# Forty single-row loads per step instead of twenty-four, in a gather-and-sum kernel on one Trainium2 core

## The chip, the cores and the metric

The kernel runs on one core of a Trainium2 chip. The metric is the device time of one execution in microseconds; the time before is the median of three executions. An execution that was recorded by the hardware profiler is one of them, and everything said of the profile below comes from it.

## The reference

A graph layer with two kinds of messages, a residual sum, and a layer norm. `x` has 50,000 rows of 128 float32 numbers, and there are 1,650,000 edges, sorted by `dst`. Every node has one edge to itself among them.

```python
Xs = X[src]
m_data = Xs @ W_data.T + b_data
m_ctrl = Xs @ W_control.T + b_control
msg = jnp.where((edge_types == 0)[:, None], m_data, m_ctrl)
agg = jax.ops.segment_sum(msg, dst, num_segments=X.shape[0])
out = jax.nn.relu(agg + (X @ W_self.T + b_self))
result = layernorm(x + out)          # over the last axis
```

## The kernel before

The edges are cut into `NBLK` blocks, in their order. A block has `Q = 2` steps, and a step has `R = 12` chunks of 128 edges. For a chunk, one indirect DMA of GpSimd (POOL, line 483) fetches the 128 source rows of `x` into an SBUF tile `y`; TensorE multiplies `y` with a one-hot matrix `oh` of 128 x 120 (60 nodes for each of the two edge types, line 502), and so sums the rows by node and type into a PSUM tile `acc`. The weights are multiplied in later, once per block (`layer`). That is float32, so each product is two weight loads and two matmuls in the trace.

A step takes more edges than its 12 x 128 = 1,536, in two ways, and both make a block longer and the number of blocks smaller:

- **Fillers.** An edge from a node to itself needs no gather, since the node's own row is there anyway (`xT`). Its place in a chunk is given to another edge, a filler. `F = 43` of these are taken in a step. VectorE (DVE) works out which place gets which filler (`fill`, lines 315 to 337; its tiles are 128 x 26 x `F`), and corrects the sums for the edges that were left out (`left_out_columns`, `_matrix`, `_numbers`, `_rows`).
- **Single rows.** `S = sum(TURNS) = 24` more edges of a step are fetched one row at a time, 512 bytes for each DMA, by the queues of SP and ACT (`single_rows`, line 457): 12 in each step for each queue, so 24 in each block for each queue. The tile is `yx`, with a row on each partition. They are the `S` rows of one more product in each step (line 508, 24 partitions x 120).

For single rows the queue first reads the row offsets from `at_x` into registers (`TENSOR_LOAD`, line 452), then for each row does a register `MOVE` and a DMA issue, both line 457. `LOADS` says in how many parts this is done in a block; a part has at most 32 rows for each queue. The rows of block `b + 2` are issued in block `b` (`AHEAD = 2`), on two semaphores, and `rows_fetched` makes PE wait for all of them before the product of line 508 in the first step of their block (line 466). There are four tiles for them (`ROW_SLOTS`).

The order on each engine is written out by hand (`manual_schedule`), in the loop over `b` at the end of `straight`. A block has four passes of six chunks, two in each step. The gathers have ten tiles (`SLOTS`) of one pass each, so GpSimd can be up to ten passes ahead of PE; it waits for PE to free a tile. In a block's program order, with `q` for the pass:

- SP: `xT` of block `b + 3` (line 408), every tenth block the edge lists (lines 167 to 172) and the fillers' lists (lines 300, 305), the single rows of block `b + 2`, and every second block two output stores (line 577).
- ACT: the single rows of block `b + 2`, and every second block the square root of two blocks' variances (`root`, line 563).
- DVE: `add` of the last step of block `b - 1` (line 518), `begin_sums` (531), `offsets` for `at_x` (437), `onehot` and `counts` of block `b + 2` (414, 422), then `fill` of block `b + 5`, `add` of the first step, `moments` of block `b - 1` and the rest.
- PE: pass 0, `left_out_columns` (344), pass 1 with lines 508 and 511, `layer` of block `b - 1` (537 to 541), `left_out_numbers` (360, 363), pass 2, pass 3 with 508 and 511.

If a step has fewer edges to itself than `F`, or if its nodes don't fit the one-hot matrix, a flag is set, and a second, general way of computing everything runs after the first.

Of the kernel before, what the change touches and what calls it, by code (L numbers as in the profile page):

```python
# [37 lines left out]
PASS = 6  # L38
B = 112
C = R * Q  # L40
F = 43
TURNS = (12, 12)
S = sum(TURNS)
LOADS = 1
BEGIN = (0, -(-Q * TURNS[0] // 4) * 4)
X = BEGIN[1] + -(-Q * TURNS[1] // 4) * 4
R1 = R + 1
# [3 lines left out]
CE = Q * SIZE  # L51
BE = CE + Q * (F + S)
NBLK = 2 + (E - CE) // BE
# [30 lines left out]
def plain(b):  # L84

    return b == 0 or b >= NBLK - 1
# [6 lines left out]
def straight(ctx, tc, c, x, x_t, edges_t, edges_f, src_x, dst_first, first_p, out):  # L93
# [35 lines left out]
                   allow_small_or_imprecise_dtypes=True)  # L129
    FILL = Q * F + C1  # L130
    small = keep_ps.tile([P, 2 * W + F + 2 * FILL + 2], F32, name="small")
    num_ps, rank_no_ps = small[:, :2 * W], small[:, 2 * W:2 * W + F]
    lists = [small[:, 2 * W + F + i * FILL:][:, :FILL] for i in range(2)]
    sums_at = [small[:Q * F, 2 * W + F + 2 * FILL + i:][:, :1] for i in range(2)]

# [282 lines left out]
    def counts(b):  # L418

        cnt = ohp.tile([P, Q, 2 * W], BF16, name="cnt")  # L420
        with nc.allow_low_precision(reason="whole numbers up to R1"):
            nc.vector.tensor_reduce(cnt, ohs[b].rearrange("p (q r) w -> p q w r", r=R1), AX.X, ALU.add)  # L422
        cnts[b] = cnt
# [15 lines left out]
    def part_of(n, part):  # L439

        return min(n, 32 * part)

    def single_rows(b, part):

        if part == 0:
            ys[b] = stp.tile([S, Q, D], F32, name="yx", bufs=ROW_SLOTS)
        both = []
        for j, (eng, dma) in enumerate(((SP, nc.sync), (ACT, nc.scalar))):
            n = Q * TURNS[j]
            k0, k1 = part_of(n, part), part_of(n, part + 1)  # L450
            at = BEGIN[j]
            _, rows = nc.values_load_multi_w_load_instructions(ats[b][0:1, at + k0:at + k1], engines=[eng], **RANGE)
            both.append([(dma, fetched[j][b % ROW_SLOTS], *divmod(k0 + k, TURNS[j]), sum(TURNS[:j]), row)
                         for k, row in enumerate(rows)])
        for pair in zip_longest(*both):
            for dma, sem, q, k, at, row in filter(None, pair):
                copy = dma.dma_start(ys[b][at + k:at + k + 1, q, :].bitcast(U8), x_bytes[:, bass.ds(row, ROW)])
                copy.then_inc(sem, 16)
                tc.no_tile_sem_insts.add(copy.ins.name)
                tc.add_to_no_dep_group(f"single{b}", copy.ins)  # L460

    def rows_fetched(b):

        times = len(range(b % ROW_SLOTS or ROW_SLOTS, b + 1, ROW_SLOTS))
        for j in range(2):
            wait = nc.tensor.wait_ge(fetched[j][b % ROW_SLOTS], 16 * Q * TURNS[j] * times)
        tc.declare_fence(wait.ins, group=f"single{b}")
# [89 lines left out]
    def pair(b):  # L557

        return range(b // 2 * 2, b + 1) if b % 2 == 1 or b == NBLK - 1 else ()
# [6 lines left out]
    def store(bs):  # L566
        mv = mvs.pop(bs[0] // 2)
        rstd = stp.tile([B, 2], F32, name="rstd")
        nc.vector.reciprocal(rstd[:, :len(bs)], sds.pop(bs[0] // 2)[:, :len(bs)])
        for i, b in enumerate(bs):  # L570
            o = stp.tile([B, D], F32, name="o", bufs=4)
            nc.vector.tensor_scalar(o, hs.pop(b), mv[:, i, 0:1], rstd[:, i:i + 1], op0=ALU.subtract, op1=ALU.mult)
            os_[b] = o
# [43 lines left out]
    for b in range(1, RAHEAD):  # L617
# [3 lines left out]
        if b < AHEAD:  # L621
            onehot(b)
            counts(b)
            for part in range(LOADS):
                single_rows(b, part)
        if b == 1:
            clear_sums()
    for b in range(NBLK + 1):
# [20 lines left out]
        for q, (step, ks) in enumerate(passes_of(b)):  # L649
# [21 lines left out]
            if q == 3 and b > 0 and pair(b - 1):  # L671
                store(pair(b - 1))
            if q < LOADS and not plain(b + AHEAD):
                single_rows(b + AHEAD, q)
# [336 lines left out]
```

## Time and profile before

| What | Value |
|---|---|
| Median of three executions | 17865.75 us (17860.93 to 17866.0) |
| Profiled execution, its own time | 17866.0 us |
| Its span, first to last instruction | 17864.2 us |
| Instructions in the span | 162923 |
| Blocks; span for each | 515; 34.69 us |
| DVE busy | 11010.2 us (62%) |
| POOL busy | 11675.7 us (65%) |
| PE busy, weight loads | 8518.6 us (48%), 7294.5 us (41%) |
| ACT busy | 79.5 us |
| DMA | 53 GB/s, 2 tenths of the 16 engines' time |

The profile lists the engines' busy time, the groups of instructions by source line, who waited for whom, and the order of time. Register, semaphore and DMA-issuing instructions aren't counted as busy: so SP has no busy time at all, and ACT almost none, though both issue DMAs for most of the span. What they do is seen in the order of time and in the instructions of their lines. A releaser "remote" means that the profile found no instruction that ended the wait. "issue" means that the engine waited for nothing the profile shows.

### The profile page before, as it was taken

How to read it: one execution, taken by the hardware profiler on the slowest of the kernel's cores; microseconds unless marked ns; L12 is line 12 of the kernel's file. 1: busy time of each engine (PE TensorE's matmuls, PEld its weight loads, DVE VectorE, ACT ScalarE, POOL GpSimd, SP SyncE). 2: the span in 40 equal slices, each digit the busy share in tenths (PEclk: the TensorE clock that was granted, in tenths of full speed). 3: DMA queues.
4: the chain of work that ended last, by engine and by line, in shares of the span. 5: the costliest groups of instructions: out<-in, count | busy, mean ns of one | idle time of the engine just before them, and what ended most of it. 6: DMA issues, size and time to landing. Idle time of an engine off the chain costs nothing.

```text
span 17864.2 us, 162923 instructions
## 1 busy us (share of the span) xinstructions
PE 8518.6 (48%) x36190; PEld 7294.5 (41%) x36191; DVE 11010.2 (62%) x13887; ACT 79.5 (0%) x264; POOL 11675.7 (65%) x12364
## 2 busy tenths in 40 slices
PE   3444444444444444444444444444444444444444
PEld 3444444444444444444444444444444444444444
DVE  6666666666666666666665656666665666666665
ACT  0000000000000000000000000000000000000000
POOL 6666666666666666666666666666666666666666
PEclk6555555555555555555555555555555555555555
DMA  2122221222122122222212222121221212122121
GB/s 55 52 53 52 53 53 52 53 52 53 52 53 53 52 53 53 52 53 52 53 52 53 53 52 53 52 54 52 53 53 52 53 52 53 52 53 53 52 53 49
DMA packets 604666, 938.00 MB, mean 53 GB/s; under 512 B 308795, under 2 KB 392578, under 8 KB 603676
## 3 DMA queue, kind: packets, MB, share of 16 engines
q0 software_dynamic: 395392, 810.40, 17.4%
q1 hardware_dynamic: 183222, 110.53, 2.4%
q10 hardware_dynamic: 25062, 6.55, 0.2%
q8 instruction: 295, 4.83, 0.1%
q14 instruction: 695, 5.69, 0.1%
HBM read 896.80 MB, written 29.71 MB: 52 GB/s over the span
## 4 chain that ended last, share of the span: by engine, by line
DVE 39%; another core or an unknown queue 30%; issue 17%; PE 13%; DVEq 1%; SPq 0%; DMA 0%; ACT 0%; ACTq 0%
DVE cnt L422 11%; PE acc L502 9%; DVE oh L414 8%; DVE new L321 3%; DVE m L318 3%; DVE v_new L325 3%; DVE old L334 2%; DVE sums L518 2%; PE acc L508 1%; PE po L541 1%; DVE h L548 1%; DVE st L550 1%; DVE by L337 1%; PE po L539 1%
## 5 line engine op out<-in xcount | busy, mean ns | idle before, releaser
L483 POOL DMA_INDIRECT y<-in_x,idx x12336 | 11656.9, 945 | 6148.3 <-issue 3460.1
L502 PEld LDWEIGHTS acc<-oh,y 128*128 128x128 f32 x24708 | 5473.5, 316 | 8928.2 <-issue 6942.1
L502 PE MATMUL acc<-oh,y 128*128 128x120 f32 x24708 | 6125.0, 413 | 5208.9 <-issue 5203.1
L518 DVE TENSOR_TENSOR sums<-acc,sums 128x180 f32 x1030 | 354.8, 344 | 4744.9 <-remote 4432.1
L422 DVE TENSOR_REDUCE cnt<-oh 128x240 bf16<-128x3120 f32 x515 | 3011.9, 5848 | 17.9
L414 DVE TENSOR_TENSOR oh<-col,small 128x3120 f32<-128x3120 f32 x515 | 1743.1, 3385 | 0.0
L344 PE MATMUL small<-ones_b,by 128*86 128x1 bf16 x513 | 84.0, 164 | 3418.4 <-issue 2299.4
L337 DVE TENSOR_REDUCE by<-old 128x86 bf16<-128x1118 f32 x513 | 1111.2, 2166 | 19.0 <-DVE old L334 1.3
L547 DVE COPY h<-po 112x128 f32<-112x128 f32 x515 | 147.6, 287 | 1378.8 <-remote 1020.1
L508 PE MATMUL acc<-oh,yx 24*128 24x120 f32 x2052 | 783.0, 478 | 81.9 <-issue 80.4
L318 DVE TENSOR_TENSOR m<-rk,small 128x1118 f32<-128x1118 f32 x513 | 677.0, 1320 | 18.0 <-issue 0.5
L321 DVE TENSOR_TENSOR new<-m,small 128x1118 f32<-128x1118 f32 x513 | 677.1, 1320 | 17.6
L325 DVE TENSOR_REDUCE v_new<-new 128x26 f32<-128x1118 f32 x513 | 675.8, 1317 | 17.6
L334 DVE TENSOR_TENSOR old<-m,small 128x1118 f32<-128x1118 f32 x513 | 672.7, 1311 | 0.0
L508 PEld LDWEIGHTS acc<-oh,yx 24*128 24x128 f32 x2052 | 502.5, 300 | 306.0 <-issue 300.3
L541 PE MATMUL po<-wmsgT,sums 128*112 128x128 f32 x2060 | 613.1, 453 | 0.0
L541 PEld LDWEIGHTS po<-wmsgT,sums 128*112 128x112 f32 x2060 | 448.8, 297 | 127.4 <-issue 126.6
L539 PE MATMUL po<-bias,sums 3*112 3x128 f32 x1030 | 391.9, 482 | 1.0 <-DVE sums L518 1.0
L538 PE MATMUL po<-wselfT,xT 128*112 128x128 f32 x1030 | 325.2, 419 | 0.0
L511 PE MATMUL acc<-cnt,to_row 128*128 128x60 bf16 x2060 | 288.7, 230 | 69.4 <-issue 69.0
L531 DVE TENSOR_TENSOR sums<-pl,sums 128x336 f32<-128x336 f32 x513 | 260.3, 507 | 83.5 <-issue 53.0
L267 PEld LDWEIGHTS <-ones_b 128*128 128x128 bf16 x624 | 78.7, 149 | 540.0 <-issue 528.5
(118 smaller groups left out, 3994.2 us busy)
## 6 DMA issues: line engine op xcount, KB each, us to landing
y<-in_x,idx POOLq DMA_INDIRECT x12336
yx<-in_x ACTq DMA_DIRECT2D x12312, 0.5 KB
yx<-in_x SPq DMA_DIRECT2D x12312, 0.5 KB
xT<-in_x_t SPq DMA_DIRECT2D x515, 56.0 KB
out<-o SPq DMA_DIRECT2D x515, 56.0 KB
vf_all<-vd SPq DMA_DIRECT2D x52, 430.0 KB
sdt<-in_edges_t SPq DMA_DIRECT2D x52, 390.0 KB
one_g<-in_src_x SPq DMA_DIRECT2D x52, 1.9 KB
```

The lines of the kernel that those rows point to most:

```text
L318: nc.vector.tensor_tensor(m, rk_g[g][:, i, :, None].to_broadcast([P, C1, F]), rank_no_ps[:, None, :].to_broadcast([P, C1, F]), op=ALU.is_e ...
L321: nc.vector.tensor_tensor(new.rearrange("p (q r) f -> p q r f", r=R1), m.rearrange("p (q r) f -> p q r f", r=R1), vf.rearrange("p (q f) -> ...
L325: nc.vector.tensor_reduce(v, new, AX.X, ALU.add)
L334: nc.vector.tensor_tensor(old, m, cb[:, :, None].to_broadcast([P, C1, F]), op=ALU.mult)
L337: nc.vector.tensor_reduce(by, old.rearrange("p (q r) f -> p q f r", r=R1), AX.X, ALU.add)
L414: nc.vector.tensor_tensor(oh, col_g[g][:, i, :, None].to_broadcast([P, C1, 2 * W]), num_ps[:, None, :].to_broadcast([P, C1, 2 * W]), op=AL ...
L422: nc.vector.tensor_reduce(cnt, ohs[b].rearrange("p (q r) w -> p q w r", r=R1), AX.X, ALU.add)
L483: copy = nc.gpsimd.indirect_dma_start(out=y[:r, k % PASS, :].bitcast(U8), out_offset=None, in_=x_rows, in_offset=bass.IndirectOffsetOnAxis ...
L502: nc.tensor.matmul(acc[:, :2, :].rearrange("p t w -> p (t w)"), y[:r, k % PASS, :], ohs[b][:r, column(k), :], start=k == of_step[0], stop= ...
L508: nc.tensor.matmul(acc[:, :2, :].rearrange("p t w -> p (t w)"), ys[b][:, q, :], ohs[b][:S, q * R1 + R, :], start=False, stop=True)
L518: nc.vector.tensor_tensor(part, accs.pop((b, q)), part, op=ALU.add)
L541: nc.tensor.matmul(po, a[:, t, :B], c["wmsgT"][:, t * D:(t + 1) * D], start=False, stop=t == 1)
```

## The change

Three constants change. Nothing else does; all shapes follow from them.

```diff
-F = 43
-TURNS = (12, 12)
+F = 42
+TURNS = (20, 20)
 S = sum(TURNS)
-LOADS = 1
+LOADS = 2
```

What follows from them:

- A step takes 1,536 + 42 + 40 = 1,618 edges instead of 1,536 + 43 + 24 = 1,603, and a block 3,236 instead of 3,206. `NBLK = 2 + (E - CE) // BE` goes from 515 to 510.
- Each of the two queues issues 40 single rows in a block instead of 24, and reads their offsets in two parts, 32 and 8, instead of one of 24. The first part is issued after pass 0 in the program's order, the second after pass 1.
- The product of line 508 has 40 partitions instead of 24. `at_x` has 80 numbers instead of 48.
- The tiles of `fill` have 128 x 26 x 42 elements instead of 128 x 26 x 43.

## The prediction

> **What bounds the kernel now.** I read the page first. No engine is full: DVE 62%, POOL 65%, PE 48%. So I asked for POOL's waits, since the gathers are the work that the blocks are made of.
>
> ```profile
> L483 POOL DMA_INDIRECT y<-in_x,idx x12336 | 11656.9, 945 | 6148.3 <-issue 3460.1
> ```
> ```profile
> POOL y L483 <- issue: 3465.3, 11355, 1.9
> POOL y L483 <- remote: 2186.4, 692, 4.9
> POOL y L483 <- PE acc L502: 220.9, 122, 10.9
> ```
>
> A gather costs 0.945 us and 0.30 us of issue behind it, 1.247 us from start to start. A block's 24 take 29.9 us, of the 34.69 us that a block lasts (17864.2 / 515). The other 4.8 us are waits, for PE to free a tile of `y`. So PE is late, although it is idle for half of the span. The order of time shows why:
>
> ```profile
> 8063.99 0.36 PE L502 MATMUL acc<-oh,y 128*128 128x120 f32 x1 [1.74 <-issue]
> 8065.39 0.36 PE L502 MATMUL acc<-oh,y 128*128 128x120 f32 x1 [1.04 <-issue]
> ...
> 8077.19 2.90 PE L502 MATMUL acc<-oh,y 128*128 128x120 f32 x12
> ```
>
> There are two paces. In the third line 12 matmuls take 2.90 us, with their weight loads beside them; in the first two, one comes every 1.4 to 2.1 us, and PE waits for nothing that the profile names. The same is seen on the queues of the single rows:
>
> ```profile
> 8002.29 2.69 ACTq L457 DMA_DIRECT2D yx<-in_x  x8
> ```
> ```profile
> 8008.37 7.00 SPq L457 DMA_DIRECT2D yx<-in_x  x5
> ```
>
> Eight rows in 2.69 us, 0.335 us each; or five in 7.00, 1.40 us each. Instruction by instruction, PE, SP and ACT then go in steps of 0.70 us, and a row is two of them, `MOVE` and issue (a `MOVE` of 0.029 us takes 0.70). What holds them isn't told by the profile. Adding up the stretches in which one of the three goes at that step gives some 12,860 us, 72% of the span, 25.0 us of a block. They end 2 to 4 us after POOL stops and begin again some 5 us after it goes on, so the slow pace goes with running gathers. Here POOL had stopped, PE came free at 8075, and this is POOL's next gather:
>
> ```profile
> 8077.05 0.94 POOL L483 DMA_INDIRECT y<-in_x,idx  x1 [4.62 <-PE acc L502]
> ```
>
> Last I read the queue that the change loads, SP, in the order of time (two blocks of it) and by its waits.
>
> ```profile
> 8154.80 25.00 SPq L457 DMA_DIRECT2D yx<-in_x  x24
> 8180.50 0.00 SPq L408 DMA_DIRECT2D xT<-in_x_t  x1
> 8180.52 0.33 SPq L305 DMA_DIRECT2D vf_all<-vd  x1
> 8182.70 32.14 SPq L457 DMA_DIRECT2D yx<-in_x  x24
> 8217.34 2.55 SPq L577 DMA_DIRECT2D out<-o  x2
> ```
> ```profile
> SPq L577 <- DVE o L572: 1068.3, 94, 35.9
> SPq L408 <- remote: 478.8, 115, 22.9
> ```
>
> SP is never counted as busy, and is nearly full. A run of 24 rows takes 26.5 us in the mean of all 513, so 1.106 us for a row. All of SP's waits together are 1,825 us, 3.5 us of a block; for the other 31.1 us it is issuing. Of these 4.6 us are not rows (`xT`, stores, register loads, lists). ACT is less full: 20.2 us for 24 rows, and it waits 12.3 us of a block in front of the square root.
>
> **The change, part by part.**
>
> *Fewer blocks.* 510 instead of 515: 5 x 34.69 = 173 us less, 0.97%, if a block lasted as long as before.
>
> *42 fillers.* Lines 318, 321, 325, 334 (1.32 us each) and 337 (2.17 us) are 1/43 shorter: 0.17 us of DVE in a block. DVE is busy for 21.4 us of 34.7 and waits 4,432 us at line 518 alone; I cost it at nothing. If DVE were the bound, it would be 510 x 0.17 = 87 us less.
>
> *The product of line 508 with 40 partitions.* With 24 partitions its weight load takes 0.300 us, and line 502's with 128 takes 0.316. Partitions cost nothing here: zero, at most 4 x 0.016 us of PE in a block.
>
> *`at_x` with 80 numbers on one partition.* 0.198 us for 48 now; line 225, the same operation with 260, takes 0.298. So +0.02 us in a block, beside DVE's waits: nothing.
>
> *The offsets in two parts.* Line 452 takes 1.42 us on SP (median) for 24 registers; line 401 reads 8 in 0.777. That is 0.04 us for a register and 0.45 us for the load. 32 and 8 are then 1.74 + 0.78 = 2.52 us: 1.1 us more on SP in a block. ACT (1.67 us now) gets about as much. The ends are 0.78 us (one more load of 8) and 1.42 (a second load of 24).
>
> *Sixteen more rows in a block on each queue.* On SP the floor is 16 x 0.335 = 5.4 us, the present mean 16 x 1.106 = 17.7 us, the slow pace 16 x 1.40 = 22.4 us. SP has 3.5 us to spare. Even at the floor 5.4 + 1.1 = 6.5 us don't fit: SP becomes the engine that sets the end. At the floor a block needs 31.1 + 6.5 = 37.6 us, at the present mean 31.1 + 17.7 + 1.1 = 49.9 us.
>
> The value is nearer to the floor. When SP is late, PE waits at line 466, ahead of line 508. Behind it in PE's queue stand `layer`, `left_out_numbers` and passes 2 and 3; DVE waits for them at lines 518 and 547, and POOL for their tiles. So POOL stops, and the time added to a block is time without gathers, which has the fast pace. POOL's 29.9 us of gathers stay, and with them some 25.0 us of slow pace in a block. In these SP issues 25.0 / 1.40 = 17.9 rows. The other 22.1 take 22.1 x 0.335 = 7.4 us, and what isn't rows takes 4.6 + 1.1 = 5.7. Together 25.0 + 7.4 + 5.7 = 38.1 us. The waits of SP go, since they are for things (`o`, a free `xT`) that are long there when SP is the late one. ACT's rows need at its mean price 40 x 0.84 + 2.8 = 36.5 us, just less. Whatever small wait stays, I add 0.4 us: 38.5 us.
>
> There is a buffer: SP's last row of a block is issued 49.5 us (median; never under 26.8) before PE's product that uses it. It delays the effect by one or two blocks of 510 and takes nothing off the sum. The bytes are no term: 32 rows are 16 KB in a block, beside 24 gathers of 64 KB. `xT` is issued over 70 us ahead, so SP's other transfers come into no trouble first.
>
> The sum: 510 x 38.5 = 19,635 us, 1,770 above the profiled execution's 17,866.0, which stands 0.25 us from the median of the runs. I take 19,640.
>
> Two rules of the Trainium skill pull in opposite directions here. *DMA: Bandwidth & Descriptors*, section Issuing engines are not separate DMA queues, says that the sequencer's time to start a DMA "is usually small relative to the DMA itself"; by that the rows cost nothing and the sum would be -173 us. *Perfetto Trace Analysis*, section What "DMA-bound" means, counts a solid track of DMA slices on the issuing sequencer as a bound of its own; that speaks against the change, and SP's 31.1 us of 34.7 are of that kind.
>
> **The rivals.**
>
> *The rows are hidden (faster).* One mechanism: the slow pace shrinks, so that SP fits 40 rows into the block it has. The point is a mean price of (34.7 - 4.6 - 1.1) / 40 = 0.725 us for a row, against 1.106 now; ACT, at 0.84 for the same instructions, shows that such prices occur. Then POOL and PE go on as before: 17,866 - 173 = 17,690, or with DVE's part 17,600. Against it: nothing in the change slows the gathers, and SP goes slowly whenever they run. 0.06.
>
> *The slow pace is a limit on the number of instructions.* If PE, SP and ACT share something with a fixed rate, a block costs by its instructions: 316 now, and 64 more with the moves and issues, +20%. 34.69 x 1.20 x 510 = 21,260. For it: the free stretches are shorter the more SP and ACT issue in them. Against it: PE goes at 0.70 us also where SP and ACT issue nothing (8057 to 8075). 0.20.
>
> *The price of a row stays.* If slow stretches go on while POOL waits, a block takes up to 49.9 us: 25,450. Stretches end within 4 us of POOL's stop, against it. 0.10.
>
> *SP absorbs part*, because the slow stretches are fewer with longer stops: 35 to 36 us, 17,850 to 18,360. 0.03.
>
> *The change doesn't do what it says*: a step with fewer than 42 edges to itself, or with over 60 nodes, would start the general way, far slower. Counted from the inputs, the least is 43 and the most nodes 55, so it stays out. 0.01.
>
> **How the numbers follow.** The main case has 0.60. Its own range is 36.1 us (the slow pace is a tenth shorter and nothing waits) to 40.5 us (half of SP's present waits stay). The range reaches from its low end, 18,400, over the second rival's 21,260 to 22,500, where part of the third lies; outside are the first rival and most of the third, less than 2 in 10. A measurement of this kernel tells 0.2% (36 us) from no change. Faster 0.06; same 0.01, from the partial case; slower 0.93.
>
> **What the profile after should show.** 508 runs of 40 rows on SP with 20,320 rows on each queue and 12,240 gathers. SP's waits fall from 1,825 us to under 600. Runs of 40 rows on SP take 30 to 33 us, so 0.75 to 0.85 us a row. POOL's waits for tiles rise from 4.8 to 8 or 9 us of a block, and PE waits ahead of line 508 for the rows. DVE's busy time falls by 1 to 2%. I am wrong if SP still has waits of 3 us in a block, if POOL waits no longer than before, or if the rows' mean price is still 1.1 us.

## The result, and the profile after

| | before | after |
|---|---|---|
| Median | 17864.68 us (4 executions, 17860.93 to 17866.0) | 19067.91 us (4 executions, 19051.4 to 19087.19) |
| Profiled execution, own time and span | 17866.0, 17864.2 us | 19051.4, 19049.7 us |
| Blocks, span for each | 515, 34.69 us | 510, 37.35 us |
| Instructions in the span | 162923 | 194872 |
| DVE, POOL, PE busy | 11010.2, 11675.7, 8518.6 us | 10857.1, 11573.3, 6914.5 us |

The changed kernel is slower: 1.0674 times the time before, with a 95% interval of 1.0656 to 1.0693. Five blocks fewer would have brought 173 us; each of the 510 that are left takes 2.66 us more. Three groups of the page after, with the idle time ahead of each:

```profile
L483 POOL DMA_INDIRECT y<-in_x,idx x12216 | 11549.2, 945 | 7415.0 <-issue 3349.5
...
L508 PE MATMUL acc<-oh,yx 40*128 40x120 f32 x2032 | 643.8, 408 | 9148.8 <-issue 6185.7
...
L315 DVE COPY small<-vf_all 128x84 f32<-128x84 f32 x508 | 123.7, 243 | 2194.2 <-DMA vf_all<-vd 1026.0
```

The second of them before the change:

```profile
L508 PE MATMUL acc<-oh,yx 24*128 24x120 f32 x2052 | 783.0, 478 | 81.9 <-issue 80.4
```

A gather still takes 945 ns. What grew is the idle time ahead of it, from 6148.3 to 7415.0 us. The big number is the one on line 508: PE stands idle for 9148.8 us, 17.9 us of a block in the mean, in front of the product that uses the single rows, where it was 81.9 us. Not all of that is added time. PE's idle time in front of line 502's matmuls fell from 5208.9 to 469.6 us, and a block is longer by only 2.66 us: for the most part PE waits in another place. "issue" is only what the profile puts down where it found no instruction that ended the wait; the other part, 2963.1 us, has PE's own queue at line 466 as its releaser, which is the wait for the rows.

POOL's waits for a tile of `y`, in the list of waits:

```profile
POOL y L483 <- issue: 3356.5, 10999, 0.6
...
POOL y L483 <- remote: 2062.7, 771, 3.9
...
POOL y L483 <- PE acc L502: 1848.1, 338, 19.1
```

The first line is the 0.30 us between gathers, as before. The last one went from 220.9 to 1848.1 us, and its longest wait from 10.9 to 19.1 us: PE frees the tiles too late, because it stands at line 508. Summed over the gathers, what lies above 1.247 us from start to start is 7.3 us in a block, against 4.8.

SP's waits by releaser, the two longest:

```profile
SPq L452 <- DVE sums L518: 106.0, 83, 2.1
SPq L577 <- DMA out<-o: 87.7, 71, 1.8
```

All together are some 430 us, 0.8 us of a block, where they were 1,825. The 1068.3 us that SP waited for `o` at line 577 are gone. SP is almost never free, so what it needs is there when it comes to it. In the order of time (SP first, then PE in the same stretch; start, duration, instructions, and in brackets the idle time before) one sees who waits for whom:

```profile
8028.66 42.06 SPq L457 DMA_DIRECT2D yx<-in_x  x40
8070.78 2.17 SPq L577 DMA_DIRECT2D out<-o  x2
...
8076.94 31.68 SPq L457 DMA_DIRECT2D yx<-in_x  x40
...
8113.59 29.39 SPq L457 DMA_DIRECT2D yx<-in_x  x40
```
```profile
8071.43 0.78 PE L508 MATMUL acc<-oh,yx 40*128 40x120 f32 x2 [26.24 <-issue]
...
8108.70 0.78 PE L508 MATMUL acc<-oh,yx 40*128 40x120 f32 x2 [21.40 <-PEq L466]
```

SP's run of 40 rows ends at 8070.72 and PE's product starts at 8071.43, after 26 idle microseconds; the next run ends at 8108.62, and PE goes on at 8108.70. Over all 508 blocks, SP's last row of a block is issued 1.3 us (median, start to start) before the product's first weight load. Before the change it was 49.8 us. On ACT the same distance is 79 us. The buffer of two blocks was used up early, and SP, not ACT, has been the late one ever since.

### The profile page after: what moved, and what is told of

It is laid out like the page before. It is cut to its first block, busy times and chain, and to the rows that moved or that the text cites. A ratio compares the mean times of both kernels' runs of the same rounds, so it can differ in the third digit from the quotient of the medians.

```text
span 19049.7 us, 194872 instructions
## 1 busy us (share of the span) xinstructions
PE 6914.5 (36%) x35844; PEld 6045.6 (32%) x35845; DVE 10857.1 (57%) x13740; ACT 78.6 (0%) x261; POOL 11573.3 (61%) x12250
## 5 line engine op out<-in xcount | busy, mean ns | idle before, releaser
L483 POOL DMA_INDIRECT y<-in_x,idx x12216 | 11549.2, 945 | 7415.0 <-issue 3349.5
L502 PEld LDWEIGHTS acc<-oh,y 128*128 128x128 f32 x24480 | 4360.8, 274 | 2791.5 <-issue 1899.4
L502 PE MATMUL acc<-oh,y 128*128 128x120 f32 x24480 | 4680.8, 366 | 469.6 <-issue 468.6
L508 PE MATMUL acc<-oh,yx 40*128 40x120 f32 x2032 | 643.8, 408 | 9148.8 <-issue 6185.7
L508 PEld LDWEIGHTS acc<-oh,yx 40*128 40x128 f32 x2032 | 405.9, 248 | 9350.8 <-issue 6284.2
L315 DVE COPY small<-vf_all 128x84 f32<-128x84 f32 x508 | 123.7, 243 | 2194.2 <-DMA vf_all<-vd 1026.0
L337 DVE TENSOR_REDUCE by<-old 128x84 bf16<-128x1092 f32 x508 | 1080.2, 2126 | 19.7 <-issue 1.4
L318 DVE TENSOR_TENSOR m<-rk,small 128x1092 f32<-128x1092 f32 x508 | 656.1, 1292 | 17.8 <-DVE small L316 0.5
L321 DVE TENSOR_TENSOR new<-m,small 128x1092 f32<-128x1092 f32 x508 | 656.1, 1292 | 17.3
L325 DVE TENSOR_REDUCE v_new<-new 128x26 f32<-128x1092 f32 x508 | 655.8, 1291 | 17.4
L334 DVE TENSOR_TENSOR old<-m,small 128x1092 f32<-128x1092 f32 x508 | 651.9, 1283 | 0.0
L369 DVE TENSOR_TENSOR pl<-pl,xT 128x224 f32<-128x224 f32 x508 | 198.6, 391 | 430.6 <-remote 235.7
```

What stands on the lines that cost most here:

```text
L318: nc.vector.tensor_tensor(m, rk_g[g][:, i, :, None].to_broadcast([P, C1, F]), rank_no_ps[:, None, :].to_broadcast([P, C1, F]), op=ALU.is_e ...
L321: nc.vector.tensor_tensor(new.rearrange("p (q r) f -> p q r f", r=R1), m.rearrange("p (q r) f -> p q r f", r=R1), vf.rearrange("p (q f) -> ...
L325: nc.vector.tensor_reduce(v, new, AX.X, ALU.add)
L334: nc.vector.tensor_tensor(old, m, cb[:, :, None].to_broadcast([P, C1, F]), op=ALU.mult)
L337: nc.vector.tensor_reduce(by, old.rearrange("p (q r) f -> p q f r", r=R1), AX.X, ALU.add)
L483: copy = nc.gpsimd.indirect_dma_start(out=y[:r, k % PASS, :].bitcast(U8), out_offset=None, in_=x_rows, in_offset=bass.IndirectOffsetOnAxis ...
```

## The experiments

The theory: SP's issuing of single rows sets the time of a block, since in the slow pace (PE, SP and ACT in steps of 0.70 us) a row costs two steps; and the slow pace goes with running gathers. The rivals: the slow pace is a limit on the number of instructions, whichever queue issues them; and ACT, nearly as full, binds as soon as SP does not.

One thing must be known to read the runs. They fell on several chips, and the kernel before has two levels: 15,458 to 15,459 us on three of them, 17,865 to 18,015 us on the others. On the first kind the steps of 0.70 us do not occur in the traces. The TensorE clock does not explain it: the kernel before was granted less of it where it took 15,459 us (0.51) than where it took 17,865 us (0.537). So each run is compared with the kernel before on its own chip, and "with steps" or "without steps" says which kind it was.

**Another split of the same 80 rows.** 34 rows for SP and 46 for ACT in a block, or the reverse; blocks, fillers and instructions are those of the changed kernel.

```diff
-TURNS = (20, 20)
+TURNS = (17, 23)      # sp34_act46;  (23, 17) in sp46_act34
```

> The changed kernel with the same 80 rows and 510 blocks, but 34 of a block's rows on SP and 46 on ACT. Theory (SP's queue sets the end of a block): six rows less on SP are 6 x 0.335 = 2.0 us of a block at the fast pace, up to 6 x 0.82 = 4.9 at the mean price after the change, until another engine binds (34.7 us, as in the kernel before). 37.35 us a block goes to 35.3 or less: 17,700 to 18,100 us, and SP's rows are issued well ahead of PE again. Rival (each instruction of any queue costs, a shared limit): the number of instructions is the same, so 19,070 us. Rival (ACT binds as soon as SP doesn't): ACT waits 7.4 us of a block now and gets 2 to 4 us more, so it shouldn't; if it does, over 18,500.

> The other way round: 46 of a block's rows on SP and 34 on ACT, the same 80 rows and 510 blocks. Theory (SP's queue): six rows more on SP, 2.0 us of a block at the fast pace, since what is added is time in which the gathers stand; 39.4 us a block, 20,080 us. At the mean price of 0.82 us a row it would be 42.3 us and 21,560. Rival (a shared limit on instructions): 19,070.

Both ran without steps: 15331.2 and 15343.44 us, against 15458.73 before (ratios 0.9918, 0.9901 to 0.9935, and 0.9925, 0.9909 to 0.9942). They tell the theory and its rivals apart no further, since the slow pace that these speak of did not occur. What the runs do show is what a row costs without it. SP in the order of time, with 34 rows in a block, and POOL's waits in the same run:

```profile
8023.27 11.77 SPq L457 DMA_DIRECT2D yx<-in_x  x34
...
8045.85 12.16 SPq L457 DMA_DIRECT2D yx<-in_x  x34
```
```profile
POOL y L483 <- issue: 3683.0, 12074, 0.3
...
POOL y L483 <- PE acc L502: 3.8, 3, 3.2
```

34 rows take 12 us instead of some 30; a row costs 0.333 us from start to start in the mean, the floor of the prediction. POOL never waits for a tile, and a block is 30.06 us long (15,328.2 / 510), just above 24 x 1.247 = 29.9: gathers and almost nothing else. Even 46 rows on SP are hidden there.

**Fewer single rows, in one load.** 32 or 16 rows for each queue in a block, 43 fillers, 513 and 518 blocks.

```diff
-F = 42
-TURNS = (20, 20)
-LOADS = 2
+F = 43
+TURNS = (16, 16)      # rows32;  (8, 8) in rows16
+LOADS = 1
```

> The kernel before with 32 rows on each queue in a block, in one load (43 fillers, 513 blocks). Theory (SP's queue): eight rows and a load of 8 less than the changed kernel, 37.35 - 2.7 - 0.8 = 33.9 us, under the 34.7 that a block takes for other reasons; so 34.7 x 513 = 17,800 us, no slower than before, and SP's waits are 0.5 to 1.5 us of a block. Rival (a row costs the same wherever it stands): halfway between 24 and 40 rows, 18,460 us.

> The kernel before with 16 rows on each queue in a block (43 fillers, 518 blocks). Theory (SP's queue binds only over some 32 rows): a block takes 34.7 us as before, 518 x 34.7 = 17,970 us, and SP waits some 12 us of a block. Rival (a row costs the same wherever it stands): 8 rows less save 0.6 us for each of the 37.35 - 34.69 = 2.7 us that 16 cost, so 33.4 us a block and 17,280 us.

> 32 rows on each queue in a block, in one load, 513 blocks, again. Without the steps of 0.70 us 15,385 us, as in the run before. With them, theory (a queue costs time only when it is full): SP needs 37.4 - 8 x 0.335 - 0.8 = 33.9 us, less than the 34.7 to 35.0 us of a block, so the time is that of the kernel before or 0.4% less (513 blocks instead of 515). Rival (each row costs alike): halfway between 24 and 40 rows, 3.5% over the kernel before.

> 16 rows on each queue in a block, 518 blocks, again. Without the steps of 0.70 us 15,540 us, as in the run before. With them, theory (a queue costs time only when it is full): as long a block as before, 0.6% over the kernel before for the 518 blocks. Rival (each row costs alike): 3.5% under the kernel before. Between them stands what the theory leaves out: with fewer instructions of SP and ACT the stretches without steps may be longer, which would make a block shorter by up to 1 us (2 to 3%).

> 32 rows on each queue in a block, in one load, 513 blocks, a third time: the two runs so far had no steps of 0.70 us, and took 15,384 us, 0.5% under the kernel before. With the steps, theory (a queue costs time only when it is full): SP needs 37.4 - 8 x 0.335 - 0.8 = 33.9 us, less than the 34.7 to 35.0 us of a block, so the time is that of the kernel before or 0.4% less. Rival (each row costs alike): halfway between 24 and 40 rows, 3.5% over the kernel before. In between, 1 to 2% over it, if SP's waits can't all be used up.

All five ran without steps. 32 rows: 15384.23, 15384.57 and 15385.34 us, each 0.9952 or 0.9953 of the kernel before (the widest interval 0.9935 to 0.9969). 16 rows: 15539.07 and 15537.92 us, 1.0052 (1.0035 to 1.0069). So the question that they were made for, at which number of rows SP becomes the late one in the slow pace, stays open. Together with the splits they give a row of numbers for the chips without steps: 518 blocks 15,538, 515 blocks 15,459, 513 blocks 15,384, 510 blocks 15,331 us. That is 30.0 us for a block at every number of rows: there a block less is worth its gathers, and the rows cost next to nothing.

**The changed kernel again, and the split beside it, with steps.**

> The changed kernel itself, again, beside the kernel before. In the four runs just made the steps of 0.70 us don't occur, and the kernel before takes 15,459 us instead of 17,865: a block lasts 30.0 us, POOL's 24 gathers of 1.247 us. Theory (SP's queue sets the end only where PE, SP and ACT go in steps of 0.70 us): without the steps 40 rows are 40 x 0.32 + 2.6 = 15.4 us of SP's queue, half of a block, so POOL sets the end and the time goes with the blocks: 15,459 x 510 / 515 = 15,310 us. With the steps it is 19,070 again, 6.7% over the kernel before. Rival (the change itself brings the delay, whatever the pace): slower by 5% or more in both cases, 16,200 us without the steps.

> The changed kernel with 34 of a block's rows on SP and 46 on ACT, again. Without the steps of 0.70 us: 15,330 us as in the run before, within 0.2% of the changed kernel. With the steps, theory (SP's queue sets the end): 35.3 us a block or less, 17,700 to 18,100 us. Rival (a shared limit on instructions): the number of instructions is that of the changed kernel, 19,070 us.

The changed kernel took 19335.22 us, against 18014.7 before on that chip: 1.0731 (1.0713 to 1.0749). The chain of work that ended last in its profile names the queue. By engine it is 46% "issue", which names nothing, 26% SP's queue, 14% PE and 8% DVE; by line:

```profile
SPq L457 23%; PE acc L502 8%; SPq L452 2%; DVE cnt L422 2%; DVE oh L414 2%; PE acc L508 2%; PE po L541 1%; ACTq L457 1%; PE po L539 1%; DMA yx<-in_x 1%; DVE m L318 1%; DVE new L321 1%; DVE v_new L325 1%; PE po L538 1%
```

(In the first profile of the changed kernel that chain could be followed over only some 22% of the span, so this one is shown.)

The split 34 and 46 took 18908.82 us, 1.0498 (1.0481 to 1.0516): 426 us less than the even split, 0.84 us of a block, where I had expected a thousand or more. The theory was right in that taking six rows from SP takes away PE's wait for them entirely:

```profile
L569 DVE RECIPROCAL rstd<-sd 112x2 f32<-112x2 f32 x255 | 42.3, 166 | 5705.9 <-ACT sd L563 3458.1
...
L508 PE MATMUL acc<-oh,yx 40*128 40x120 f32 x2032 | 704.1, 440 | 59.8 <-issue 59.7
```

9488.7 us of idle time at line 508, in the even split on the same chip, have become 59.8, and SP's last row is now issued 22.6 us ahead (median). But the first line of the two is new. ACT's queue has the square root (line 563) behind its rows, every second block, and DVE waits for that. ACT, DVE and PE of this run in the order of time:

```profile
8044.64 63.24 ACTq L457 DMA_DIRECT2D yx<-in_x  x93
8107.91 0.29 ACT L563 ACTIVATE sd<-mv,eps 112x2 f32<-112x2 f32 x1 [63.63 <-issue]
```
```profile
8108.24 0.17 DVE L569 RECIPROCAL rstd<-sd 112x2 f32<-112x2 f32 x1 [18.26 <-issue]
```
```profile
8113.44 0.16 PE L344 MATMUL small<-ones_b,by 128*84 128x1 bf16 x1 [19.18 <-issue]
```

ACT issues 93 rows without a break until 8107.88, then the root; 0.33 us later DVE goes on after 18 idle microseconds, and when it has done `onehot`, PE goes on after 19. ACT, which waited 7.9 us of a block at line 563 with 40 rows, waits 0.1 us there with 46. Its price for a row rose from 0.67 us (27.0 us for a run of 40) to 0.74 (33.9 for 46), so it got 6.9 us more to issue where I had allowed 2 to 4. This is the second rival, and I had sized its room from ACT's price in the changed kernel, which did not hold. That ACT now sets the end is read from this trace; no run takes the square root off its queue. And SP, with six rows less, is as full as before: it waits 0.7 us of a block (354 us in all), and a row costs it 0.94 us. So little was to be had by balance, and a full queue is not always the late one: SP's rows are 22.6 us early here.

**Half of the gathers.** The single rows stay as in the changed kernel; every second gather is left out.

```diff
-        for k in ks:
+        for k in ks[::2]:
...
-        seen[i] += 16 * len(ks)
+        seen[i] += 16 * len(ks[::2])
...
-  y[:r, k % PASS, :]
+  y[:r, k % PASS // 2 * 2, :]
```

> The changed kernel with half of the gathers left out: of each pair of chunks only the first is fetched, and both products use its rows. Everything else stays, 40 rows on each queue included. Theory (the steps of 0.70 us go with running gathers, and SP's queue sets the end): POOL's gathers take 15.0 us of a block instead of 29.9, so the slow stretches are some 12.5 us; in them SP issues 9 rows, the other 31 take 10.4 us and the rest of SP's work 5.7: 28.6 us a block, 14,600 us. Rival (the steps have nothing to do with the gathers): SP still needs 33 us for its rows and 37 us for a block, 19,000 us. Without the steps, DVE's 21.3 us of work set the end: 11,000 to 11,500 us.

> The changed kernel with half of the gathers left out (each fetched chunk is multiplied twice), again: the run before had no steps of 0.70 us, and took 11,156 us. With the steps, theory (they go with running gathers, and SP's queue sets the end): 14,600 us. Rival (the steps have nothing to do with the gathers): 19,000 us. Without the steps 11,156 us again.

> The changed kernel itself, a third time. With the steps of 0.70 us 7% over the kernel before, as in both runs so far. Without them, theory (POOL's gathers set the end, and SP's queue is half empty): 510 blocks instead of 515, 15,459 x 510 / 515 = 15,310 us, about 0.9% under the kernel before; the two kernels with 34 and 46 rows on SP took 15,331 and 15,343. Rival (the change itself brings the delay, whatever the pace): 5% or more over the kernel before.

Without steps it took 11156.08 us, within what was expected, and another engine is the bound there, DVE:

```profile
PE 6764.9 (61%) x35844; PEld 6006.7 (54%) x35845; DVE 10774.5 (97%) x13740; ACT 78.6 (1%) x261; POOL 5782.2 (52%) x6130
```

With steps it took 12726.17 us in its one execution, beside 19118.6 for the changed kernel on the same chip (1.0694 of the kernel before, 1.0676 to 1.0712). The page, and SP in the order of time:

```profile
L483 POOL DMA_INDIRECT y<-in_x,idx x6108 | 5797.0, 949 | 6858.0 <-PE acc L502 3617.9
...
L508 PE MATMUL acc<-oh,yx 40*128 40x120 f32 x2032 | 639.4, 406 | 3643.9 <-PEq L466 2858.4
```
```profile
8025.16 22.36 SPq L457 DMA_DIRECT2D yx<-in_x  x40
...
8051.50 20.27 SPq L457 DMA_DIRECT2D yx<-in_x  x40
```

SP is still the late one: it waits 1.6 us of a block (793 us in all), PE waits for its rows at line 508, and its last row comes 1.5 us ahead of the product. But the same 40 rows take 20.4 us (mean over the blocks) instead of 32.8: 0.51 us for a row instead of 0.82, though not one row, move or load was taken out. So the price of a row follows the gathers (or the bytes that they move: both were halved). The size was off again, by 1,900 us below the 14,600 expected, as the next part shows: the slow stretches shrank more than the gathers did.

## Why the prediction was right or wrong

The direction and the mechanism were right: SP's rows do not fit into the block, SP becomes the engine that sets the end, PE waits ahead of line 508, and POOL then waits for tiles. The time, 19,068 us, is 2.9% under the 19,640 that I took and inside the main case's own range (37.35 us of a block, of 36.1 to 40.5).

The sum of SP's block can now be set against the trace. The times below run from the start of one instruction of SP to the start of the next, so that they add up to the block; "slow" is what starts inside a stretch in which one of PE, SP and ACT goes at the 0.70-us step.

| SP, us of a block | predicted | measured |
|---|---|---|
| rows in slow stretches | 17.9 x 1.40 = 25.0 | 14.2 x 1.52 = 21.7 |
| rows outside | 22.1 x 0.335 = 7.4 | 25.6 x 0.408 = 10.4 |
| what isn't rows, with the waits left | 5.7 + 0.4 = 6.1 | 5.2 |
| sum | 38.5 | 37.35 |

*The slow stretches* are the mis-sized term. I kept them at 25.0 us of a block because the gathers stay. They came to 11,077 us in all, 21.7 us of a block, against 12,856 before, with 1% fewer gathers. Per microsecond of POOL's gathers that is 0.96, and before 1.10; in the split 34 and 46 it is 1.14, and with half of the gathers 0.67 (3,887 us by 5,797). These counts depend on where a stretch is taken to begin and end: with another rule (at least two gaps within 0.05 us of 0.70, 1.40 or 2.10, with nothing between them but gaps under 0.05 us) the four kernels have 13,372 (before), 11,736 (after), 13,016 (34 and 46) and 3,823 us (half), up to 6% off. So "the slow pace goes with running gathers" holds as a direction, shown by the half, and does not hold as a constant. What sets the ratio stays open; stops of POOL by more than 3 us are about as many (472, and 445 before).

*The rows outside the stretches* were too cheap: 0.408 us for a row and not the floor of 0.335. More rows at that price gave back 3.0 of the 3.3 us. The run of 40 rows, 32.8 us, thus came out at the upper end of the 30 to 33 us foretold, and the mean price at 0.82 of 0.75 to 0.85, by two errors that cancel, which is luck. Of the 1.15 us by which the sum for a block was too high, only 0.3 are the rows'; 0.9 are the next term's.

*The floor.* The 37.6 us that the prediction gave as a block's least time "at the floor" was no floor: a block took 37.35. It kept the 24 rows that were there already at 1.106 us each, and the shorter slow stretches made these cheaper too.

*What isn't rows.* The second load was priced well: line 452 takes 2.55 us of a block for its two loads, 1.33 before, so 1.2 against 1.1 foretold. The rest fell from about 3 us to about 2, which fits `xT` and the stores being hit by the steps less often; that I had left as it was. The waits fell to 430 us, foretold under 600.

*ACT* was said to need 36.5 us. It needed about 29 of 37.35, as its price fell to 0.67 for a row. It stood in nobody's way, so the error cost nothing here; it would have, had the rows been split otherwise.

*Other transfers.* "SP's other transfers come into no trouble first" was half wrong. `xT` is in none, but the fillers' lists are issued by SP too, and DVE now waits at line 315 for `vf_all`: 1026.0 us by that name and 984.5 by "remote", where it was 132.9 in all. DVE has room for it, and the traces do not show that it moved the end.

*POOL's waits* were to be 8 or 9 us of a block and are 7.3, as the block is shorter. *DVE's busy time* fell by 1.4%, foretold 1 to 2.

The rivals. *The price stays* (25,450 us) is out, by the 0.82. *A limit on instructions*: with 20% more of them in a block it asked for 21,260 us, and got 19,068; and the split 34 and 46, with the same 194,872 instructions, took 426 us less. Instructions in a microsecond were 9.1 before, 10.2 after and 14.8 with half of the gathers, so there is no fixed rate. That the queues share something is not excluded by this: ACT's price rose when the end no longer waited for SP. *The rows are hidden* is what the chips without steps show for the same rows split otherwise: 0.8% less, near the 0.97% of that rival. The even split itself was not run there, so for it this is argued from both neighbours, not shown. *SP absorbs part* (35 to 36 us of a block) had the right idea of the stretches, which did shrink by 3.3 us of a block, but SP's rows outside them cost more than it could allow.

On the two rules: the one of *DMA: Bandwidth & Descriptors*, section Issuing engines are not separate DMA queues, by which the sequencer's time is "usually small relative to the DMA itself", led to a sum of -173 us. That fits the outcome on the chips without steps, where 34 rows at 0.333 us are 11.3 of a block's 30.06 us and hidden; how long a row's own transfer takes, with which the sentence compares, was not measured. With steps the other held, of *Perfetto Trace Analysis*, section What "DMA-bound" means: SP issued for 36.5 of 37.35 us, and that was the bound. But a solid track alone did not tell it: with 34 rows SP issued for 36.3 of 37.04 us and was not the late one. The distance from SP's last row to the product that uses it (1.3 us, against 22.6) did.

## What to carry to other kernels

An engine that the busy list does not show can be the fullest one: before work is put on a queue, add up its waits, since what it still waits for is the room it has at today's prices (3.5 us here, for rows that needed 6.5 at the cheapest price in the trace). Then ask by how much its work comes ahead of the engine that uses it, because a full queue whose work comes early costs nothing. A mean price taken from a trace is not a constant: the same row cost 1.11, 0.82, 0.51 and 0.33 us in four runs of this case, so give a floor and a ceiling and ask what happens to the price when the new bound stops the others. And when a second queue has the same kind of work, see what stands behind its rows (here a square root that DVE needs) before its idle time is counted as room.

## What the runs showed of the hardware that was not expected

- The steps of 0.70 us do not come from the kernel alone. The kernel before took 15,458 to 15,459 us on three chips, and 17,865, 17,881 and 18,015 us in the three sets of runs on the others; the traces of the second kind have the steps, those of the first do not. The change is slower on the second kind (1.0674, 1.0731 and 1.0694), and the same rows split otherwise are faster on the first (0.9918 and 0.9925). All runs on one chip were of one kind, but each chip on record was used for one set of runs only, so the chip and the time at which it was used can't be told apart, and no run tells what makes the steps.
- Where they occur they go with indirect gathers: with half of the gathers, 31% of the span instead of 58% lies in such stretches. The gather itself is not slower, 945 to 949 ns in every run.
- A single row of 512 bytes costs a queue 0.33 us at best, a `MOVE` and an issue, and about 1.5 us from start to start inside such a stretch (about 1.1 with half of the gathers).
